# Attention over neighbour lists: the sums of a block's weights added by GpSimd in place of VectorE, with running least and greatest sums for the guard

## The chip, the cores and the metric

The kernel runs on one core of one Trainium2 chip. The metric is the device time of one execution in microseconds. A profiled execution gives the trace; the times are those of executions without a profile.

## The reference

Four graph layers run one after the other on the same graph of 2048 nodes (`adj` is a 0/1 matrix in which about one entry in 128 is set) and on 8 batch entries with 128 features per node. Layers 0 and 1 are multi-head attention over the neighbours with a feed-forward part; layers 2 and 3 are graph attention with additive scores. Only neighbours count in each softmax.

```python
# layers 0 and 1
Q = (h @ Wq).reshape(B, N, 8, 16); K = ...; V = ...
scores = jnp.einsum('bnhd,bmhd->bhnm', Q, K) / jnp.sqrt(16)
scores = jnp.where(adj == 0, -jnp.inf, scores)
attn = jax.nn.softmax(scores, axis=-1)
attn_out = jnp.einsum('bhnm,bmhd->bnhd', attn, V).reshape(B, N, 128)
x = layer_norm(h + (attn_out @ Wo + bo))
x = layer_norm(x + relu(x @ W1 + b1) @ W2 + b2)
# layers 2 and 3
h = x @ W
e = leaky_relu((h @ a_src)[:, :, None] + (h @ a_dst)[:, None, :], 0.2)
att = softmax(jnp.where(adj == 0, -jnp.inf, e), axis=-1)
x = layer_norm(att @ h + x)
```

## The kernel before

**Lists and blocks.** The kernel first finds each node's neighbours, sorts the nodes by their number of neighbours and cuts them into 16 blocks of 128 nodes, one node per partition. A block t has as many slots as its longest list may need (`CAPS`: 28 plus 2 folded ones for block 0, then 23, 21, 20, 19, 18, 18, 17, 16, 16, 15, 14, 14, 13, 12, 11). In each layer a table in HBM holds one row per node: key and value of all 8 batch entries in layers 0 and 1 (2048 columns), projected features and two exponentials in layers 2 and 3 (1040 columns). For slot k of block t, one indirect DMA of GpSimd's queue (`gather`, L319) fetches the table rows of the k-th neighbours of the block's 128 nodes into a buffer `kv`, of which there are six (`KVB`).

**Chunks.** The work is cut into chunks of 2 slots (layers 0 and 1) or 4 slots (layers 2 and 3). A chunk of attention goes through these steps in `attention_chunk`:

- VectorE multiplies the keys by the queries `q` (L640, 128 x 2048 elements) and adds halves of the products once or twice (L645);
- TensorE sums what is left into the PSUM tile `pair` (L648), and ScalarE takes the exponential into the weights `w`, 64 columns per slot (8 batch entries x 8 heads, L653);
- VectorE multiplies the values by the weights (L659);
- TensorE adds the weighted values of all slots into the PSUM accumulator `acc` (L326, through `add_up`). After that the buffer is free, and the gather of the chunk six places on may go.

**The sums.** The softmax needs the sum of `w` over a block's slots. When a block's last chunk is due to be weighted, `sums` calls `reciprocal_sums`, which adds the slots by halves on VectorE (L467, in place, the last step L469), adds the folded part in block 0, reduces the 64 sums to their least and greatest value (L476, L477, kept in one column of `dmin` and `dmax` per layer and block) and inverts them (L478). At the very end `verdict` reduces `dmin` and `dmax` and sets a flag; if a sum was out of bounds, a general path would compute everything anew. Layers 2 and 3 use the same function with one reduction (L471) over 8 columns.

**Order.** No scheduler moves instructions: the order in which the program is written is each engine's order. The main loop `layers` runs over the chunks i and interleaves three ages: products of chunk i, sums and weighting of chunk i-2, accumulation of chunk i-3. Between them it calls `slot()` three times a chunk. A slot moves every generator in `threads` and `tails` on by one `yield` and lets `fetch` issue gathers up to three chunks ahead (four in layers 2 and 3). So a chunk's gather stands on GpSimd's queue at the start of the round three chunks earlier.

`scales` (a thread begun right after the sums) spreads the inverted sums over the features on ScalarE and transposes them on TensorE. `tail` waits four slots (layers 0 and 1) after the last accumulation and then calls `outputs` (L678: accumulator times scale) and begins `attention_tail`: output projection, norm, feed-forward part, norm, and the next layer's rows. When both halves of a block are done, `state_done` writes the state back (SP's queue) and scatters the rows into the next layer's table (`put_rows`, L515, GpSimd's queue). The first chunks of the next layer use lists sorted such that they need only the first 13, 14 or 15 blocks of the new table (`EARLY`); all later ones need all 16, and `fetch` holds their gathers back until those writes have been issued. If a chunk's gather isn't issued when its turn comes, the loop calls empty slots until it is:

```python
            while i < len(every) and now[1] <= i:
                slot()
```

Of the kernel before, what the change touches and what calls it, by code (L numbers as in the profile page):

```python
# [8 lines left out]
F32 = mybir.dt.float32  # L9
# [5 lines left out]
ALU = mybir.AluOpType  # L15
AX = mybir.AxisListType

P = 128
B, N, D = 8, 2048, 128
NT = N // P  # L20
NH = 8
# [7 lines left out]
NB = 8  # L29
# [9 lines left out]
BASE, MANY, FOLD = 28, 16, 2  # L39
CAPS = [BASE + FOLD, 23, 21, 20, 19, 18, 18, 17, 16, 16, 15, 14, 14, 13, 12, 11]  # L40
# [44 lines left out]
def sparse_path(ctx: ExitStack, tc: tile.TileContext, ins: dict, out: bass.AP, flag: bass.AP):  # L85
# [10 lines left out]
    nc = tc.nc  # L96
    const = ctx.enter_context(tc.tile_pool(name="const", bufs=1))
    work = ctx.enter_context(tc.tile_pool(name="work", bufs=2))
    small = ctx.enter_context(tc.tile_pool(name="small", bufs=2))
# [5 lines left out]
    def misc():  # L105
        return pm.tile([P, 512], F32, tag="m", name="m")
# [51 lines left out]
    score = const.tile([P, 2, NT, 2 * B], F32, name="score")  # L158
    over = const.tile([P, 2, NT], F32, name="over")
    found = dram.tile([N, N // SEG * 8], F32, name="found")  # L160
    dmin = const.tile([P, 4, NT], F32, name="dmin")
    dmax = const.tile([P, 4, NT], F32, name="dmax")

# [159 lines left out]
    def turn_into(dst, src, start):  # L325
        nc.tensor.matmul(  # L326
            dst, src, ident, start=start, stop=True, is_transpose=True, skip_group_check=True
        )
# [127 lines left out]
        box["folded"] = small.tile([P, columns], F32, tag="folded", name="folded", bufs=1)  # L456
        nc.scalar.copy(box["folded"], ps)

    def reciprocal_sums(l, t, w, columns, folded):

        sums = small.tile([P, columns], F32, tag="sums", name="sums")
        n = CAPS[t] if t > 0 else BASE
        if l < 2:

            while n > 2:
                m = -(-n // 2)
                nc.vector.tensor_add(w[:, : n - m, :], w[:, : n - m, :], w[:, m:n, :])  # L467
                n = m
            nc.vector.tensor_add(sums, w[:, 0, :], w[:, 1, :])  # L469
        else:  # L470
            nc.vector.tensor_reduce(  # L471
                sums, w[:, :n, :].rearrange("p s c -> p c s"), axis=AX.X, op=ALU.add
            )
        if t == 0:
            nc.vector.tensor_add(sums, sums, folded)
        nc.vector.tensor_reduce(dmin[:, l, t : t + 1], sums, axis=AX.X, op=ALU.min)  # L476
        nc.vector.tensor_reduce(dmax[:, l, t : t + 1], sums, axis=AX.X, op=ALU.max)  # L477
        nc.vector.reciprocal(sums, sums)  # L478
        return sums

# [188 lines left out]
            yield  # L669

    def sums(l, t, box):
        box["r"] = reciprocal_sums(l, t, box["w"], NB * (NH if l < 2 else 1), box.get("folded"))

    def outputs(l, t, box):
        acc, scale = box["acc"], box["scale"]
        box["o"] = o = work.tile([P, NB, P], F32, tag="o", name="o", bufs=1)
        for i in range(0, NB, 4):
            nc.vector.tensor_mul(o[:, i : i + 4, :], acc[:, i : i + 4, :], scale[:, i : i + 4, :])  # L678

    def scales(l, box):  # L680

        box["scale"] = scale = work.tile([P, NB, P], F32, tag="oT", name="scale", bufs=1)
        if l < 2:
            r = box["r"].rearrange("p (b h) -> p b h", h=NH)
            nc.scalar.copy(
                scale.rearrange("p b (j h) -> p b j h", h=NH),
                r[:, :, None, :].to_broadcast([P, NB, HD, NH]),
            )
            yield
        for i in range(0, NB, 4):  # L690
            pt = misc()
            for j in range(4):
                r = box["r"][:, i + j : i + j + 1].to_broadcast([P, P])
                turn_into(pt[:, j * P : (j + 1) * P], scale[:, i + j, :] if l < 2 else r, j == 0)
            yield
            nc.scalar.copy(scale[:, i : i + 4, :].rearrange("p b n -> p (b n)"), pt)
# [378 lines left out]
    def verdict():  # L1075
        ok = small.tile([P, 5], F32, tag="ok", name="ok", bufs=1)
        every = score.rearrange("p a t b -> p (a t b)")
        nc.vector.tensor_reduce(ok[:, 3:4], every, axis=AX.X, op=ALU.max)
        nc.vector.tensor_reduce(ok[:, 4:5], every, axis=AX.X, op=ALU.min)
        nc.vector.tensor_single_scalar(ok[:, 3:4], ok[:, 3:4], SCORE_MAX, op=ALU.is_le)  # L1080
        nc.vector.tensor_single_scalar(ok[:, 4:5], ok[:, 4:5], -SCORE_MAX, op=ALU.is_ge)
        nc.vector.tensor_mul(ok[:, 3:4], ok[:, 3:4], ok[:, 4:5])
        nc.vector.tensor_reduce(ok[:, 0:1], dmin.rearrange("p a b -> p (a b)"), axis=AX.X, op=ALU.min)
        nc.vector.tensor_reduce(ok[:, 1:2], dmax.rearrange("p a b -> p (a b)"), axis=AX.X, op=ALU.max)
        nc.vector.tensor_reduce(ok[:, 2:3], over.rearrange("p a b -> p (a b)"), axis=AX.X, op=ALU.max)
        nc.vector.tensor_single_scalar(ok[:, 0:1], ok[:, 0:1], SUM_MIN, op=ALU.is_ge)
        nc.vector.tensor_single_scalar(ok[:, 1:2], ok[:, 1:2], SUM_MAX, op=ALU.is_le)
        nc.vector.tensor_single_scalar(ok[:, 2:3], ok[:, 2:3], 0.0, op=ALU.is_le)
        nc.vector.tensor_mul(ok[:, 0:1], ok[:, 0:1], ok[:, 1:2])
        nc.vector.tensor_mul(ok[:, 0:1], ok[:, 0:1], ok[:, 2:3])  # L1090
        nc.vector.tensor_mul(ok[:, 0:1], ok[:, 0:1], ok[:, 3:4])
        pk = misc()
        nc.tensor.matmul(pk[:1, :1], ok[:, 0:1], onesc, start=True, stop=True)
        bad = small.tile([1, 1], I32, tag="bad", name="bad", bufs=1)
        nc.vector.tensor_scalar(bad, pk[:1, :1], -1.0, float(P), op0=ALU.mult, op1=ALU.add)
        nc.sync.dma_start(flag, bad)
# [8 lines left out]
    for l in range(4):  # L1105
        per = 2 if l < 2 else 4
        for t, k, ns, folded in pieces(l, per):
            c = dict(l=l, t=t, k=k, ns=ns, folded=folded, box=blocks[l][t])
# [48 lines left out]
    def later(n, make):  # L1157
        for _ in range(n):
            yield
        yield from make()  # L1160

    def tail(l, t, box):
        for _ in range(4 if l < 2 else 3 if t > NT - 4 else 5):
            yield
        outputs(l, t, box)
        if l < 2:
            tails.append(later(1, lambda: attention_tail(l, t, box, 0)))
            tails.append(later(4, lambda: attention_tail(l, t, box, 4)))
        else:
            tails.append(later(1, lambda: gat_tail(l, t, box)))  # L1170
        yield
# [19 lines left out]
    def layers():  # L1191
# [9 lines left out]
        for i in range(len(every) + 2):  # L1201
            c1, c, n1, n2 = (chunk(i + j) for j in range(-1, 3))
            while added:
                c2 = added.pop(0)
                go(c2)
                if c2["last"]:
                    threads.append(tail(c2["l"], c2["t"], c2["box"]))
# [23 lines left out]
            if c1["l"] in (2, 3) and c1["last"]:  # L1231
                sums(c1["l"], c1["t"], c1["box"])
                threads.append(scales(c1["l"], c1["box"]))
# [6 lines left out]
            while weighed and len(weighed) > (2 if c["l"] in (0, 1) else 0):  # L1240
                c2 = weighed.pop(0)
                if c2["last"]:
                    sums(c2["l"], c2["t"], c2["box"])
                    threads.append(scales(c2["l"], c2["box"]))
                go(c2, 2)
                added.append(c2)
            if c1["l"] in (2, 3):
                go(c1, 2)
                if c1["last"]:
                    threads.append(tail(c1["l"], c1["t"], c1["box"]))  # L1250
            slot()
        verdict()
        drain()

# [528 lines left out]
```

## Time and profile before

| | us |
|---|---|
| median of 3 runs | 3161.54 |
| lowest and highest | 3149.05, 3168.8 |
| profiled execution, its own time | 3022.89 |
| span of its trace | 3021.1 |
| VectorE (DVE) busy in the span | 2743.3 |
| TensorE (PE) busy | 2517.4 |
| GpSimd (POOL) busy | 1784.3 |
| ScalarE (ACT) busy | 1379.7 |

The profiled execution was faster than all three timed ones. Durations below come from its trace. In a group of the profile, the columns are line, engine, operation, tiles, shapes and count, then the busy time in us and the mean of one in ns, then the engine's idle time before these instructions and what ended it. A row of a timeline has start, length, engine, line, operation, tiles, shapes and, in brackets, the idle time before it. L319 is line 319 of the kernel before. The attention layers take about 215 to 1140 us and 1140 to 2090 us of the span, and layers 2 and 3 the rest.

### The profile page before, as it was taken

The numbers are of one execution on the slowest core, as the hardware profiler recorded it, in microseconds if no ns is written. First come the engines' busy times: TensorE is split into PE (matmuls) and PEld (weight loads), VectorE is DVE, ScalarE is ACT, GpSimd is POOL, SyncE is SP. The second block draws the span as 40 slices with busy tenths as digits, with TensorE's granted clock in tenths as the row PEclk, the third lists the DMA queues.
The fourth block names the chain that finished last, engine by engine and source line by source line (L and its number), as shares of the span: only waits on it lengthen the run. The fifth ranks groups of instructions, "written<-read, shape, count | busy, mean of one in ns | idle before, by whom it ended". The sixth has DMA issues, their size and how long they took to land.

```text
span 3021.1 us, 52130 instructions
## 1 busy us (share of the span) xinstructions
PE 2517.4 (83%) x19258; PEld 2320.8 (77%) x19258; DVE 2743.3 (91%) x2945; ACT 1379.7 (46%) x4898; POOL 1784.3 (59%) x1293
## 2 busy tenths in 40 slices
PE   5756888789889999688888898999678898788886
PEld 3646777778788898677888788888578888687786
DVE  8788999999999998999999999998599998499996
ACT  4721333444445555043444454545345556244454
POOL 0057578677755644545546555554577775477773
PEclk8978999999999999899999999999798899899998
DMA  8688889988988887778888889886799999799995
GB/s 331 234 301 320 310 310 324 347 299 314 362 304 335 313 305 316 279 260 343 307 322 325 344 323 333 322 309 241 259 395 403 397 414 355 261 411 412 409 412 216
DMA packets 200692, 987.63 MB, mean 327 GB/s; under 512 B 31918, under 2 KB 33712, under 8 KB 128436
## 3 DMA queue, kind: packets, MB, share of 16 engines
q0 software_dynamic: 175024, 890.45, 77.7%
q1 hardware_dynamic: 20502, 75.52, 6.5%
q10 hardware_dynamic: 4904, 18.24, 1.9%
q8 instruction: 155, 2.54, 0.3%
q14 instruction: 107, 0.88, 0.1%
HBM read 937.16 MB, written 91.55 MB: 341 GB/s over the span
## 4 chain that ended last, share of the span: by engine, by line
PE 36%; DVE 30%; DMA 16%; issue 9%; ACT 5%; POOL 1%; POOLq 0%; DVEq 0%; ACTq 0%
PE acc L326 12%; DMA kv<-table,lists 11%; DVE kv L640 9%; DVE kv L659 8%; PE pair L648 5%; DVE kv L645 4%; DMA kv<-table,sorted_lists 3%; PE m L752 3%; DVE kv L797 3%; PE m L731 2%; PE m L533 2%; PE m L333 2%; DMA table<-rows,perm 2%; PE m L557 1%; PE m L548 1%
## 5 line engine op out<-in xcount | busy, mean ns | idle before, releaser
L319 POOL DMA_INDIRECT kv<-table,lists x955 | 1334.0, 1397 | 764.8 <-PE acc L326 491.9
L326 PE MATMUL acc<-ident,kv 128*128 128x128 f32 x8208 | 1059.8, 285 | 180.0 <-DVE kv L659 98.4
L326 PEld LDWEIGHTS acc<-ident,kv 128*128 128x128 f32 x8208 | 978.2, 148 | 258.7 <-DVE kv L659 120.5
L640 DVE TENSOR_TENSOR kv<-kv,q 128x2048 f32<-128x2048 f32 (+1 forms) x282 | 629.2, 2231 | 46.5 <-DMA kv<-table,lists 18.7
L659 DVE TENSOR_TENSOR kv<-kv,w 128x2048 f32<-128x2048 f32 (+1 forms) x284 | 632.4, 2227 | 0.0
L648 PE MATMUL pair<-kv,ident 128*128 128x128 f32 (+1 forms) x3344 | 444.3, 284 | 141.5 <-issue 66.7
L797 DVE TENSOR_TENSOR kv<-kv,pair 128x3584 f32<-128x3584 f32 (+1 forms) x150 | 540.0, 3600 | 1.9
L648 PEld LDWEIGHTS pair<-kv,ident 128*128 128x128 f32 x3344 | 411.7, 197 | 167.1 <-issue 100.3
L653 ACT ACTIVATE w<-pair,lmask 128x64 f32<-128x64 f32 x554 | 144.7, 311 | 738.8 <-PE pair L648 738.7
L645 DVE TENSOR_TENSOR kv<-kv 128x1024 f32<-128x1024 f32 (+1 forms) x434 | 442.5, 1020 | 14.3
L494 ACT ACTIVATE n<-m,eps 128x128 f32<-128x128 f32 x512 | 181.5, 367 | 296.8 <-PE m L718 154.3
L319 POOL DMA_INDIRECT kv<-table,sorted_lists x153 | 188.4, 1231 | 126.3 <-PE acc L326 56.6
L802 ACT ACTIVATE kv<-kv,ws 128x128 f32<-128x128 f32 x554 | 177.9, 400 | 180.6 <-DVE ws L791 173.9
L844 ACT ACTIVATE n<-m,eps 128x128 f32<-128x128 f32 x256 | 90.8, 374 | 183.1 <-PE m L836 183.1
L515 POOL DMA_INDIRECT table<-rows,perm x57 | 85.1, 1493 | 132.9 <-ACT score L568 31.4
L752 PE MATMUL m<-w_L_w,hT 128*128 128x128 f32 x1024 | 156.2, 275 | 0.0
L501 ACT ACTIVATE n<-m,rs 128x128 f32<-128x128 f32 x512 | 146.3, 376 | 1.1
L752 PEld LDWEIGHTS m<-w_L_w,hT 128*128 128x128 f32 x1024 | 134.9, 192 | 0.0
L731 PE MATMUL m<-n1T,w_L_gnn_W 128*128 128x512 f32 x256 | 131.5, 597 | 0.6 <-ACT q L606 0.6
L333 PE MATMUL m<-ident,n 128*128 128x128 f32 x640 | 107.8, 291 | 11.9 <-ACT rows L562 7.5
L678 DVE TENSOR_TENSOR o<-acc,scale 128x512 f32<-128x512 f32 x128 | 82.9, 683 | 37.6 <-PE acc L326 23.3
L333 PEld LDWEIGHTS m<-ident,n 128*128 128x128 f32 x640 | 83.4, 151 | 36.2 <-issue 14.7
(238 smaller groups left out, 3615.4 us busy)
## 6 DMA issues: line engine op xcount, KB each, us to landing
kept<-xT SPq DMA_DIRECT2D x48, 512.0 KB, 6.2
xT<-kept SPq DMA_DIRECT2D x48, 512.0 KB, 7.5
kv<-in_adj_dram SPq DMA_DIRECT2D x16, 1024.0 KB, 6.5
table<-kv ACTq DMA_DIRECT2D x16, 1024.0 KB, 5.7
kv<-table,lists POOLq DMA_INDIRECT x955, 8.6
kv<-in_x_nodes_dram SPq DMA_DIRECT2D x16, 512.0 KB, 12.5
kv<-table,sorted_lists POOLq DMA_INDIRECT x153, 6.9
found<-cand POOLq DMA_DIRECT2D x16, 64.0 KB, 4.3
```

What stands on the lines that cost most here:

```text
L319: nc.gpsimd.indirect_dma_start(out=dst, out_offset=None, in_=tables[l][:, :], in_offset=bass.IndirectOffsetOnAxis(ap=index, axis=0), bound ...
L326: nc.tensor.matmul(dst, src, ident, start=start, stop=True, is_transpose=True, skip_group_check=True)
L333: nc.tensor.transpose(pt[:, j * P : (j + 1) * P], src[:, j, :], ident)
L494: nc.scalar.activation(dst[:, i, :], z[:, i, :], AF.Square, bias=eps, scale=D**-0.5, accum_out=ss[:, i : i + 1],)
L640: nc.vector.tensor_mul(kk, kk, q[:, None].to_broadcast([P, ns, NB, D]))
L645: nc.vector.tensor_add(kk[:, :, :, :width], kk[:, :, :, :width], kk[:, :, :, width : 2 * width])
L648: nc.tensor.matmul(sc, ident, kk[:, :, :, j : j + NH], start=j == 0, stop=j + NH == width)
L659: nc.vector.tensor_mul(vv, vv, w[:, k : k + ns, :].rearrange("p s (b h) -> p (s b) h", h=NH)[:, :, None, :] .to_broadcast([P, ns * NB, HD, ...
L731: nc.tensor.matmul(ph, wt["1"][:, f * P : (f + 1) * P], n1T.rearrange("p b c -> p (b c)"), start=True, stop=True,)
L752: nc.tensor.matmul(y[:, j, :], hT[:, f, j, :], wt["2"][:, f, :], start=False, stop=f == 1, skip_group_check=True,)
L797: nc.vector.tensor_mul(hv[:, :, :nv, :], hv[:, :, :nv, :], wc[:, :, :nv, None].to_broadcast([P, ns, nv, D]))
L802: nc.scalar.mul(hv[:, i, b, :], hv[:, i, b, :], ws[:, i, b - nv : b - nv + 1])
```

## The change

For layers 0 and 1 the sums of the weights move to GpSimd: a new function `attention_sums` does the same additions by halves in the same order with GpSimd's `tensor_add`, on GpSimd's queue, where the gathers stand. It neither reduces nor inverts. Instead `scales` waits three slots and then does three operations on VectorE: it takes the element-wise minimum of the 64 sums with a tile `least`, the maximum with a tile `most`, and the reciprocal. `least` and `most` start at 1 and run over all blocks of both layers. In `verdict` they are merged into the smaller `dmin` and `dmax`, which layers 2 and 3 still fill as before. `tail` waits seven slots in place of four in layers 0 and 1.

```diff
-    dmin = const.tile([P, 4, NT], F32, name="dmin")
-    dmax = const.tile([P, 4, NT], F32, name="dmax")
+    dmin = const.tile([P, 2, NT], F32, name="dmin")
+    dmax = const.tile([P, 2, NT], F32, name="dmax")
+    least = const.tile([P, NB * NH], F32, name="least")
+    most = const.tile([P, NB * NH], F32, name="most")
+    nc.vector.memset(least, 1.0)
+    nc.vector.memset(most, 1.0)
...
-    def reciprocal_sums(l, t, w, columns, folded):
-
-        sums = small.tile([P, columns], F32, tag="sums", name="sums")
+    def attention_sums(t, w, folded):
+
+        sums = small.tile([P, NB * NH], F32, tag="sums", name="sums")
         n = CAPS[t] if t > 0 else BASE
-        if l < 2:
-
-            while n > 2:
-                m = -(-n // 2)
-                nc.vector.tensor_add(w[:, : n - m, :], w[:, : n - m, :], w[:, m:n, :])
-                n = m
-            nc.vector.tensor_add(sums, w[:, 0, :], w[:, 1, :])
-        else:
-            nc.vector.tensor_reduce(
-                sums, w[:, :n, :].rearrange("p s c -> p c s"), axis=AX.X, op=ALU.add
-            )
+        add = nc.gpsimd.tensor_add
+        while n > 2:
+            m = -(-n // 2)
+            add(w[:, : n - m, :], w[:, : n - m, :], w[:, m:n, :])
+            n = m
+        add(sums, w[:, 0, :], w[:, 1, :])
+        if t == 0:
+            add(sums, sums, folded)
+        return sums
+
+    def reciprocal_sums(l, t, w, folded):
+
+        sums = small.tile([P, NB], F32, tag="sums", name="sums")
+        n = CAPS[t] if t > 0 else BASE
+        nc.vector.tensor_reduce(
+            sums, w[:, :n, :].rearrange("p s c -> p c s"), axis=AX.X, op=ALU.add
+        )
         if t == 0:
             nc.vector.tensor_add(sums, sums, folded)
-        nc.vector.tensor_reduce(dmin[:, l, t : t + 1], sums, axis=AX.X, op=ALU.min)
-        nc.vector.tensor_reduce(dmax[:, l, t : t + 1], sums, axis=AX.X, op=ALU.max)
+        nc.vector.tensor_reduce(dmin[:, l - 2, t : t + 1], sums, axis=AX.X, op=ALU.min)
+        nc.vector.tensor_reduce(dmax[:, l - 2, t : t + 1], sums, axis=AX.X, op=ALU.max)
         nc.vector.reciprocal(sums, sums)
         return sums
...
     def sums(l, t, box):
-        box["r"] = reciprocal_sums(l, t, box["w"], NB * (NH if l < 2 else 1), box.get("folded"))
+        if l < 2:
+            box["r"] = attention_sums(t, box["w"], box.get("folded"))
+        else:
+            box["r"] = reciprocal_sums(l, t, box["w"], box.get("folded"))
...
     def scales(l, box):
 
+        if l < 2:
+            for _ in range(3):
+                yield
+            nc.vector.tensor_tensor(least, least, box["r"], op=ALU.min)
+            nc.vector.tensor_max(most, most, box["r"])
+            nc.vector.reciprocal(box["r"], box["r"])
...
+        dmin2, dmax2 = (d.rearrange("p a b -> p (a b)") for d in (dmin, dmax))
+        nc.vector.tensor_tensor(dmin2, dmin2, least[:, : 2 * NT], op=ALU.min)
+        nc.vector.tensor_tensor(dmin2, dmin2, least[:, 2 * NT :], op=ALU.min)
+        nc.vector.tensor_tensor(dmax2, dmax2, most[:, : 2 * NT], op=ALU.max)
+        nc.vector.tensor_tensor(dmax2, dmax2, most[:, 2 * NT :], op=ALU.max)
...
     def tail(l, t, box):
-        for _ in range(4 if l < 2 else 3 if t > NT - 4 else 5):
+        for _ in range(7 if l < 2 else 3 if t > NT - 4 else 5):
             yield
```

## The prediction

> **What bounds the kernel now.** I read the page's busy totals first, then busy time by stage, then VectorE's groups with shapes kept apart, then VectorE's waits, and last the timelines of VectorE and GpSimd beside each other.
>
> ```profile
> PE 2517.4 (83%) x19258; PEld 2320.8 (77%) x19258; DVE 2743.3 (91%) x2945; ACT 1379.7 (46%) x4898; POOL 1784.3 (59%) x1293
> ...
> 215.00:1140.00 925.00, 795.63 (x6077) 727.25 (x6077) 892.51 (x796) 396.25 (x1356) 618.08 (x364) 0.97 0.86 319
> 1140.00:2090.00 950.00, 839.67 (x6624) 774.14 (x6623) 893.27 (x660) 408.46 (x1534) 508.59 (x298) 0.97 0.83 311
> ```
>
> The two rows are the two attention layers (columns: stretch, length, PE, PE loads, DVE, ACT, POOL, clock, DMA share, GB/s). VectorE is busy 892.5 of 925 us and 893.3 of 950 us, 96% and 94%. TensorE follows at 86% and 88%, the DMA engines at 86% and 83%. So VectorE sets the pace there, with two others 8 to 12 points behind. VectorE's waits in this stretch say the same: the largest row is 20.5 us in 16 waits for gathered rows, the next 14.0 us.
>
> ```profile
> L659 DVE TENSOR_TENSOR kv<-kv,w 128x2048 f32<-128x2048 f32 x270 | 616.2, 2282 | 0.0
> L640 DVE TENSOR_TENSOR kv<-kv,q 128x2048 f32<-128x2048 f32 x268 | 612.1, 2284 | 46.5 <-DMA kv<-table,lists 18.7 <-DMA kv<-table,sorted_lists 13.8 <-ACT q L606 13.3
> ...
> L478 DVE RECIPROCAL sums<-sums 128x64 f32<-128x64 f32 x32 | 17.7, 553 | 1.1
> ...
> L469 DVE TENSOR_TENSOR sums<-w 128x64 f32<-128x64 f32 x32 | 7.2, 225 | 1.1
> ...
> L476 DVE TENSOR_REDUCE dmin<-sums 128x1 f32<-128x64 f32 x32 | 7.0, 220 | 1.1
> L477 DVE TENSOR_REDUCE dmax<-sums 128x1 f32<-128x64 f32 x32 | 6.7, 209 | 0.0
> ```
>
> These are the products that fill VectorE, and the small operations that the change touches. All the products have two inputs in SBUF. Whether that matters to GpSimd is to be seen where GpSimd's gathers (POOL) stand beside VectorE:
>
> ```profile
> 1018.53 2.23 DVE L659 TENSOR_TENSOR kv<-kv,w 128x2048 f32<-128x2048 f32 x1
> 1020.68 2.28 DVE L640 TENSOR_TENSOR kv<-kv,q 128x2048 f32<-128x2048 f32 x1
> 1024.86 2.28 DVE L659 TENSOR_TENSOR kv<-kv,w 128x2048 f32<-128x2048 f32 x1
> 1027.06 2.28 DVE L640 TENSOR_TENSOR kv<-kv,q 128x2048 f32<-128x2048 f32 x1
> ...
> 1019.22 2.39 POOL L319 DMA_INDIRECT kv<-table,lists  x1 [2.25 <-PE acc L326]
> 1025.35 2.66 POOL L319 DMA_INDIRECT kv<-table,lists  x1 [1.53 <-PE acc L326]
> ...
> 2166.12 3.89 DVE L797 TENSOR_TENSOR kv<-kv,pair 128x3584 f32<-128x3584 f32 x1
> 2167.67 0.99 POOL L319 DMA_INDIRECT kv<-table,sorted_lists  x1 [0.30 <-PE acc L326]
> 2168.97 0.99 POOL L319 DMA_INDIRECT kv<-table,sorted_lists  x1 [0.30 <-issue]
> ```
>
> The first two gathers start in the middle of a product and end at 1021.61 and 1028.01, which is 0.93 and 0.95 us after the *next* VectorE instruction began (1020.68, 1027.06). They stood still until the running product was over. The last two run under a product whose second input, `pair`, lies in PSUM, and take 0.99 us. Counted over 240 to 2090 us, 328 of the 552 gathers take over 1.2 us, and 278 of these end 0.82 to 0.98 us after a VectorE start. So a GpSimd instruction that reads SBUF waits out a VectorE product with two SBUF inputs.
>
> **What the Trainium skill says.** "SBUF — State Buffer", section "Who interferes with whom": a VectorE instruction with two SBUF inputs contends with a GpSimd instruction that reads SBUF; the one that starts first keeps the shared read port for the whole instruction and the other is blocked. The trace agrees for VectorE first (above). It has no long GpSimd read, so the other direction is not shown. "GPSIMD Engine Reference", section 3.1: an fp32 add of 2048 elements takes 4497 ns on GpSimd, about 2.6 cycles at 1.2 GHz per element, 2293 ns on VectorE. The trace has 2284 ns for VectorE and no add on GpSimd. "Perfetto Trace Analysis", section "Optimizing Scalar/DVE Operations", warns that moving work between these two might not help as they share a read port.
>
> **The change part by part.**
>
> *Removed from VectorE.* 32 blocks (2 layers, 16 blocks). The rows of L467 (112 adds, 64 to 896 columns, 225 to 1096 ns) sum to 50.7 us; with L469's 7.2 the tree costs 57.9 us. The two reductions to one column cost 7.0 + 6.7 = 13.7 us.
>
> *Added to VectorE.* A running minimum and maximum of 64 columns per block: 64 instructions like L469's 225 ns, 14.4 us. The reciprocal stays (553 ns), three rounds later. The guard's four operations at the end and two fills at the start are under 2 us. Net 57.9 + 13.7 - 14.4 = 57.2 us off VectorE, 1.8 us a block.
>
> *Added to GpSimd.* 146 adds. A block of n neighbours needs n-1 sums of 64 columns; over the 16 sizes (275 neighbours) that is 259 x 64 x 2 = 33,152 elements per partition. At 2.17 ns (2.6 cycles, an estimate from GPSIMD Engine Reference) 72 us, and for each instruction 60 ns (what 4497 ns leaves) to 250 ns: 81 to 108 us in all, about 2.9 us a block. GpSimd idles 33% and 46% in these layers, so there is room.
>
> *What the adds do to VectorE.* This cost is unknown. From below: zero, if VectorE does not stand still for them; then the 57.2 us are a gain. From above: the whole 81 to 108 us, since 94 to 96% of VectorE's time is filled, mostly with two-input products. I take the block to hold in both directions, as the page says, and 95 us, of which a tenth falls on VectorE's idle time or on operations with one SBUF input: 86 us. Net on VectorE: 86 - 57 = +29 us.
>
> *Waiting at the running minimum.* On GpSimd the adds stand between the gathers of chunk i+3 and of chunk i+4. They come when VectorE starts the weighting (L659) of chunk i-2. VectorE reaches the new minimum after L659, L640, one or two L645 and L659: 2.28 x 3 + 1.6 = 8.4 us. The chain needs 4 or 5 turns, each waiting for the product in progress and then adding: four turns take about 2.2 + 2.3 + 1.4 + 2.3 for the products and 2.7 for the adds, 10.9 us against 8.4 + 2.5 (VectorE stands for the same adds). It is about even; a fifth add finishes while VectorE waits at the minimum, 0.3 us. Behind that wait stand the next L640 and everything after it. I take 0.3 x 32 = 10 us; 0 to 60.
>
> *Gathers behind the adds.* The gather of chunk i+4 (free to go at 1019.2 in the example) goes some 7 us later, when the adds end. It lands 8.6 us after its issue (page, part 6), about 1037 to 1040, and its product starts at 1041.65. That just fits; bounds 0 and 3 us a block (96 us). I take 0.
>
> *Three rounds more before the tail.* Scaling and outputs come three rounds (one chunk) later in each block. Inside a layer this is only latency. At the layer ends the new rows of the last blocks are awaited: VectorE idles 5.28 us at 1237 and 18.36 us at 2160 until a gather that follows the last table write (1224.94 and 2147.35). Each grows by one chunk, 6.3 us (L640 + L645 + L659) and 5.6 us (L797 + L808 + 0.5). Counted in the program's own loop, the empty rounds before that second gather rise from 3 to 12. Sum +12 us. On GpSimd's queue the table writes and the gathers of x fall one chunk later against the gathers; SP's order does not change.
>
> *Sum.* 29 + 10 + 12 = +51 us on the profiled execution (3022.89 us), so 3074. The median of the runs is 3161.54, 4.6% above that execution; I put the same 51 us on it: 3213 us.
>
> **The rivals.**
>
> *B, the adds do not hold VectorE.* GpSimd has the room. Then VectorE loses 57 us, the layer ends cost 12: -45 us, 3117. TensorE at 86 to 88% and DMA at 83 to 86% may keep some back, so 3117 to 3150. The point: as long as the adds hold VectorE for less than 57 - 12 = 45 of their 95 us, the kernel gains. For it: no row of before shows VectorE standing for a gather. Against: a gather reads one index per partition, too short to show it. Chance 0.22.
>
> *C, the gathers fall behind.* One mechanism: the chain of adds, taking turns with the products, keeps GpSimd's in-order queue for over 11 us a block, and chunk i+4's rows land after they are wanted. It decides from about 11 us on (1041.65 - 8.6 - two gathers of 2.4 = 1028, against 1017 for the start). At 3 us a block it adds 96 us: 3310; at half that 3260. Against: GpSimd catches up, its 46% of idle time in the second layer. Chance 0.2.
>
> *D, no net difference.* The adds hold the port for only part of their time (about 50 of 95 us): 50 - 57 + 12 and up to 10 at the minimum, 3165 to 3177. Chance 0.15.
>
> **How the numbers follow.** The forecast has 0.43, the rivals 0.22, 0.2 and 0.15. The forecast's own range is 3190 to 3245. The range that holds 8 in 10 reaches from B's bulk, 3120, to C's lower half, 3280. A measurement of this kernel tells about 1% (32 us) from no change. Faster by more than that: three quarters of B, 0.17. Within: the rest of B, D and the lower edge of the forecast, 0.23. Slower: 0.60.
>
> **What would show it.** In the trace after: L640 and L659 longer than 2.28 us, or gaps before them, where GpSimd adds; each add starting at the end of a VectorE product; GpSimd's adds near 95 us in sum; a wait of VectorE at the minimum under 1 us a block; the waits for `table2` rows near 24 us. If the products keep 2.28 us with no gaps, B is right. If VectorE's waits for `lists` rise from 20.5 us to about 100, it is C.

## The result and the profile after

The changed kernel takes 3241.40 us (median of 6 runs) where the kernel before takes 3165.77 us: 2.5% slower, ratio 1.0251 (95% interval 1.0223 to 1.0279). A second comparison of the same two kernels on another chip gave 3125.84 us against 3023.39 us, ratio 1.0326 (1.0304 to 1.0348). Chips differ: on some the kernel before takes about 3030 us, on others about 3150 us, and the trace of before shown above came from one of the first kind. So ratios below are within one chip, and traces are set beside each other only where both kernels ran on chips of one kind, or the text says otherwise. Two runs, slower than the others of their kernel, are left out of the numbers below: 4018.84 us at a granted clock of 0.62 in the last experiment, and 3199.34 us with the adds on VectorE.

Two such traces are the kernel before once more and the changed kernel once more (L650, L655 and L669 are the former L640, L645 and L659, L323 is the gather, L691 the output product). The rows give busy time by stage: attention layers 0 and 1, then layer 2; columns as in the prediction. The first three rows are of before:

```profile
177.90:1132.60 954.70, 809.09 (x6158) 741.40 (x6159) 920.43 (x833) 394.64 (x1351) 644.18 (x378) 0.96 0.87 322
1132.60:2090.80 958.20, 842.60 (x6598) 776.70 (x6597) 894.86 (x654) 407.84 (x1531) 495.25 (x293) 0.96 0.82 308
2090.80:2571.00 480.20, 394.51 (x3039) 371.33 (x3038) 417.47 (x481) 255.34 (x1013) 329.24 (x299) 0.90 0.94 362
```

and these of the changed kernel:

```profile
177.10:1176.20 999.10, 839.72 (x6131) 769.59 (x6132) 903.63 (x763) 390.33 (x1336) 681.02 (x446) 0.91 0.83 307
1176.20:2154.20 978.00, 857.90 (x6601) 789.69 (x6600) 884.37 (x582) 406.35 (x1531) 551.02 (x370) 0.94 0.81 302
2154.20:2664.20 510.00, 403.48 (x3093) 377.89 (x3092) 416.33 (x478) 262.27 (x1043) 329.30 (x300) 0.90 0.89 341
```

The attention layers grew by 64.2 us (999.1 + 978.0 against 954.7 + 958.2), layer 2 by 29.8, layer 3 by nothing (461.7 us in both). Against the trace of before that stands ahead of the prediction (953.3 + 947.3 us) the attention layers grew by 76.5 us: two executions of one kernel differ by 12 us there. In the attention layers VectorE is busy 27 us *less* (1788.0 against 1815.3) and idle 91 us more. What fills the idle time stands in VectorE's groups, here of the first trace of the changed kernel (a chip of the other kind), shapes kept apart:

```profile
L669 DVE TENSOR_TENSOR kv<-kv,w 128x2048 f32<-128x2048 f32 x270 | 632.4, 2342 | 0.0
...
L698 DVE TENSOR_TENSOR least<-least,sums 128x64 f32<-128x64 f32 x32 | 7.2, 225 | 120.7 <-POOL sums L472 116.5 <-POOL sums L474 4.2
L699 DVE TENSOR_TENSOR most<-most,sums 128x64 f32<-128x64 f32 x32 | 7.0, 219 | 0.0
```

VectorE waits 120.7 us, 3.8 us a block, at the running minimum for GpSimd's last add (116.4 us in the second trace). The weighting products went from 2282 to 2342 ns: they are held, but only a little. Summed over all VectorE instructions of the attention layers, the time above the median of each instruction's form is 26 us (29 in the second trace) against 1 us before. This sum is what "held" means below. One size of GpSimd's adds, in the same trace:

```profile
L470 POOL TENSOR_TENSOR w<-w 128x128 f32<-128x128 f32 x24 | 18.6, 777 | 1.9
```

All 146 adds take 139.7 us; at the shortest length of each size (0.32 us for 64 columns, 1.14 for 448, 2.08 for 896) it would be 97 us. The rest, 43 us, comes where adds run beside VectorE's products: those above take 777 ns on average, 453 undisturbed. Two blocks show both parts. In the first, VectorE and then GpSimd:

```profile
1069.69 2.77 DVE L655 TENSOR_TENSOR kv<-kv 128x1024 f32<-128x1024 f32 x2
1072.38 2.67 DVE L669 TENSOR_TENSOR kv<-kv,w 128x2048 f32<-128x2048 f32 x1
1075.81 0.23 DVE L698 TENSOR_TENSOR least<-least,sums 128x64 f32<-128x64 f32 x1 [0.75 <-POOL sums L472]
...
1070.54 4.84 POOL L470 TENSOR_TENSOR w<-w 128x448 f32<-128x448 f32 x3
```

The pair of L655 takes 2.77 us in place of 1.95, the product 2.67 in place of 2.28: here adds hold VectorE for 1.2 us. In the other block nothing is held, and VectorE stands still:

```profile
457.88 2.28 DVE L669 TENSOR_TENSOR kv<-kv,w 128x2048 f32<-128x2048 f32 x1
468.94 0.23 DVE L698 TENSOR_TENSOR least<-least,sums 128x64 f32<-128x64 f32 x1 [8.78 <-POOL sums L472]
...
458.46 2.60 POOL L323 DMA_INDIRECT kv<-table,lists  x1 [0.30 <-issue]
461.37 1.00 POOL L323 DMA_INDIRECT kv<-table,lists  x1 [0.31 <-issue]
462.67 1.00 POOL L417 DMA_INDIRECT place<-ranks,lists  x1 [0.30 <-issue]
463.98 0.97 POOL L344 DMA_INDIRECT xs<-in_x_nodes_dram,perm  x1 [0.30 <-issue]
464.97 3.54 POOL L470 TENSOR_TENSOR w<-w 128x640 f32<-128x640 f32 x4
468.59 0.32 POOL L472 TENSOR_TENSOR sums<-w 128x64 f32<-128x64 f32 x1
```

When VectorE comes to the minimum (460.16), GpSimd is issuing one DMA and has three more ahead of the adds. The adds themselves then run undisturbed.

### The profile page after: what moved, and what is told of

Same layout as the page of the kernel before. It is cut to its first block, busy times and chain, and to the rows that moved or that the text cites. A ratio compares the mean times of both kernels' runs of the same rounds, so it can differ in the third digit from the quotient of the medians.

```text
span 3241.3 us, 52176 instructions
## 1 busy us (share of the span) xinstructions
PE 2634.5 (81%) x19258; PEld 2404.9 (74%) x19258; DVE 2715.9 (84%) x2805; ACT 1377.8 (43%) x4898; POOL 1867.7 (58%) x1439
## 5 line engine op out<-in xcount | busy, mean ns | idle before, releaser
L323 POOL DMA_INDIRECT kv<-table,lists x955 | 1309.1, 1371 | 866.3 <-PE acc L330 515.6
L330 PE MATMUL acc<-ident,kv 128*128 128x128 f32 x8208 | 1093.2, 288 | 194.0 <-issue 84.5
L330 PEld LDWEIGHTS acc<-ident,kv 128*128 128x128 f32 x8208 | 997.9, 150 | 281.7 <-issue 153.9
L650 DVE TENSOR_TENSOR kv<-kv,q 128x2048 f32<-128x2048 f32 (+1 forms) x282 | 627.5, 2225 | 55.5 <-DMA kv<-table,lists 23.9
L669 DVE TENSOR_TENSOR kv<-kv,w 128x2048 f32<-128x2048 f32 (+1 forms) x284 | 649.6, 2288 | 0.0
L658 PE MATMUL pair<-kv,ident 128*128 128x128 f32 (+1 forms) x3344 | 465.2, 293 | 145.3 <-issue 73.5
L658 PEld LDWEIGHTS pair<-kv,ident 128*128 128x128 f32 x3344 | 432.6, 206 | 167.3 <-issue 110.2
L655 DVE TENSOR_TENSOR kv<-kv 128x1024 f32<-128x1024 f32 (+1 forms) x434 | 452.7, 1043 | 14.3
L323 POOL DMA_INDIRECT kv<-table,sorted_lists x153 | 187.7, 1227 | 132.6 <-PE acc L330 52.7
L337 PE MATMUL m<-ident,n 128*128 128x128 f32 x640 | 120.7, 299 | 26.6 <-ACT n L871 12.3
L827 DVE TENSOR_TENSOR kv<-kv 128x1024 f32<-128x1024 f32 x75 | 91.5, 1220 | 59.2 <-ACT kv L821 56.4
```

Source lines behind the costliest of these rows:

```text
L323: nc.gpsimd.indirect_dma_start(out=dst, out_offset=None, in_=tables[l][:, :], in_offset=bass.IndirectOffsetOnAxis(ap=index, axis=0), bound ...
L330: nc.tensor.matmul(dst, src, ident, start=start, stop=True, is_transpose=True, skip_group_check=True)
L337: nc.tensor.transpose(pt[:, j * P : (j + 1) * P], src[:, j, :], ident)
L650: nc.vector.tensor_mul(kk, kk, q[:, None].to_broadcast([P, ns, NB, D]))
L655: nc.vector.tensor_add(kk[:, :, :, :width], kk[:, :, :, :width], kk[:, :, :, width : 2 * width])
L658: nc.tensor.matmul(sc, ident, kk[:, :, :, j : j + NH], start=j == 0, stop=j + NH == width)
```

## The experiments

Three readings stood at the start: the wait at the minimum is the cost (W); the adds cost VectorE their own time wherever they fall (H); the later tails are the cost (L). The gain or loss of each run is against the kernel before on the same chip. The times expected in the first four were worked out from 3166 us for the kernel before, which takes 3150.83 us on their chip, so the ratios decide.

**The minimum one chunk later.**

```diff
         if l < 2:
-            for _ in range(3):
+            for _ in range(6):
                 yield
...
     def tail(l, t, box):
-        for _ in range(7 if l < 2 else 3 if t > NT - 4 else 5):
+        for _ in range(8 if l < 2 else 3 if t > NT - 4 else 5):
```

> The changed kernel with the running minimum three slots (one chunk) later: scales waits 6 slots in place of 3, tail 8 in place of 7. In the trace of the changed kernel VectorE waits 120.7 us at the minimum for GpSimd's last add, and its products and adds are lengthened by only about 24 us. Theory W (the wait is the cost, GpSimd comes late to its adds): the wait falls to under 15 us and nothing takes its place: about 3241 - 110 = 3130 us. Rival H (the adds cost VectorE their own time wherever they fall; before, most of them fell into the wait): with VectorE busy, the products are lengthened by 60 to 97 us in place of 24: 3241 - 110 + 35 to 75 = 3165 to 3205 us. Rival L (the later tail and the layer ends are the cost): one slot more of tail, so as slow as the changed kernel or slower, 3240 to 3250.

Measured 3225.15 us, ratio 1.0244 (1.0196 to 1.0292). VectorE's waits in the attention layers, first of the changed kernel, then of this one (who waits, for whom, then us in total, times, longest):

```profile
DVE least L698 <- POOL sums L472: 106.5, 27, 8.8
DVE kv L650 <- DMA kv<-table,lists: 29.6, 12, 5.7
...
DVE kv L650 <- DMA kv<-table,lists: 65.6, 38, 5.6
DVE least L698 <- POOL sums L472: 26.9, 18, 3.8
DVE o L691 <- ACT scale L715: 18.0, 23, 3.4
```

The wait at the minimum shrank to 27 us in these layers, and the time did not follow. The waits for gathered rows more than doubled, the scales came late, and the held time rose from 26 to 44 us. Neither W (3130 us) nor H (3165 to 3205) is met: the lateness moved. By its ratio the kernel is as slow as the changed one, as L had it; what the later tails cost by themselves is measured below.

**The adds ahead of the gather.**

```diff
-            box["r"] = attention_sums(t, box["w"], box.get("folded"))
+            if "r" not in box:
+                box["r"] = attention_sums(t, box["w"], box.get("folded"))
...
             now[0] = i
+            if weighed and weighed[0]["last"] and len(weighed) > (1 if c["l"] in (0, 1) else 0):
+                c2 = weighed[0]
+                c2["box"]["r"] = attention_sums(c2["t"], c2["box"]["w"], c2["box"].get("folded"))
             fetch()
```

> The changed kernel with the adds issued at the start of the round, ahead of the gather of chunk i+3 on GpSimd's queue and not behind it; everything else as changed. Theory W: GpSimd no longer stands behind a gather that waits for an accumulation, so the adds end before VectorE reaches the minimum; the wait falls from 120.7 us to under 30 and the time to 3241 - 95 = 3145 us. Rival H: the adds now meet products, whose lengthening rises from 24 to 60 to 97 us: 3180 to 3220 us. A gather that comes late behind the adds would show as a longer wait of VectorE for kv than before (20.5 us in the list gathers of before).

Measured 3265.00 us, ratio 1.0352 (1.0303 to 1.0401), the slowest of all and slower than W and H had it. Waits of this kernel in the attention layers (L699 is the minimum here):

```profile
DVE kv L650 <- DMA kv<-table,lists: 101.3, 52, 6.4
DVE least L699 <- POOL sums L472: 22.1, 18, 5.8
```

The adds now begin 3.2 us after the weighting of their chunk has begun, in place of 8.8, and the wait at the minimum has shrunk to 22 us, as W said. But what stands behind them is the gather, and VectorE waits 101.3 us for its rows; 54 us are held. With the run before, this shows that W alone is wrong: GpSimd's queue is late, and whoever is second in it is waited for.

**The adds alone, with nobody waiting for them.** The sums stay on VectorE as before; beside them GpSimd does the same number of adds, of the same sizes, on a tile of its own.

```diff
+            k = n
+            while k > 2:
+                m = -(-k // 2)
+                nc.gpsimd.tensor_add(shadow[:, : k - m, :], shadow[:, : k - m, :], shadow[:, : k - m, :])
+                k = m
+            nc.gpsimd.tensor_add(shadow[:, 0, :], shadow[:, 0, :], shadow[:, 0, :])
...
```

> The kernel before, its sums still on VectorE, and beside them on GpSimd's queue the same number of adds with the same column counts on a private tile of zeros, for whose result nobody waits. Theory W: an add that nobody waits for costs only what it holds VectorE in the changed kernel, about 24 us: 3166 + 24 = 3190 us. Rival H: the adds hold VectorE for nearly their whole uncontended time of 97 us: 3240 to 3265 us. If adds and products don't contend at all: 3166 us.

Measured 3212.10 us, ratio 1.0199 (1.0157 to 1.0240): 61 us, between W (+24) and H (+74 to 99). 43 us are held time, and waits for list rows are 65.2 us. The same kernel on a chip of the other kind:

> The shadow adds once more (144 adds beside the sums on VectorE, nobody waits for them), on one chip with the changed kernel, because the fills (+0.6%) and the few shadow adds (+1.5%) ran on another chip than the first shadow adds (+2.0%). Expected if the chip does not matter to the ratio: +1.9 to 2.1%, with VectorE lengthened by about 43 us and some 30 us of idle time more in the attention layers. If the late gathers were that chip's: nearer to +1.5%.

Measured 3095.12 us, ratio 1.0234 (1.0217 to 1.0251), again 43 us held. So adds that give VectorE nothing to wait for still cost 61 to 72 us.

**The kernel before, once more**, to tell the chips apart.

> The kernel before, once more, for a trace whose layers 2 and 3 are like those of the other traces: in the first trace of before they took 480 and 463 us, in the traces since 540 to 584 and 511 to 519, though no edit touches them. Expected of all theories: the attention layers again 953 and 947 us (within 5), layers 2 and 3 together 1050 to 1105 us.

One run, 3034.58 us. Layers 2 and 3 took 480.2 and 461.7 us, not the 1050 to 1105 together that was expected: the difference came with the chip. The two runs of the shadow adds show the same, 1056.5 us for these layers on one chip and 945.2 on the other. The second attention layer took 958.2 us where 947 (within 5) was expected.

**The same queue time without reads.** Each shadow add became two fills.

```diff
...
-                nc.gpsimd.tensor_add(shadow[:, : k - m, :], shadow[:, : k - m, :], shadow[:, : k - m, :])
+                for _ in range(2):
+                    nc.gpsimd.memset(shadow[:, : k - m, :], 0.0)
```

> The kernel before, and at the places of the shadow adds GpSimd writes zeros instead: two fills of the same columns for each add, which occupy its queue for about as long (some 88 us in all by the fill of 64 columns at 141 ns and of 128 at 204 ns, against 97 us of adds) and read nothing from SBUF. Shadow adds cost +73 us in the attention layers (43 us of lengthened VectorE instructions and 30 us more idle time). Theory P (the read port is behind both parts: adds hold VectorE, and VectorE's products hold the adds, so that these take 220 us of GpSimd's queue in place of 97 and make gathers late): fills cost next to nothing, 0 to 12 us. Rival Q (GpSimd's queue is too full for 90 us more of whatever work): VectorE is not lengthened but its waits for gathered rows grow as with the adds, +25 to 35 us.

Measured 3050.69 us against 3030.85, ratio 1.0063 (1.0040 to 1.0087): 20 us, between P and Q. GpSimd's work and VectorE's weighting product in this kernel, then in the second run of the shadow adds:

```profile
L470 POOL MEMSET shadow<- 128x64 f32 (+11 forms) x288 | 84.3, 293 | 14.7
L667 DVE TENSOR_TENSOR kv<-kv,w 128x2048 f32<-128x2048 f32 x270 | 616.6, 2284 | 0.0
...
L469 POOL TENSOR_TENSOR shadow<-shadow 128x128 f32<-128x128 f32 (+10 forms) x112 | 170.9, 1525 | 7.1
L471 POOL TENSOR_TENSOR shadow<-shadow 128x64 f32<-128x64 f32 x32 | 48.6, 1518 | 2.5
L667 DVE TENSOR_TENSOR kv<-kv,w 128x2048 f32<-128x2048 f32 x270 | 629.8, 2333 | 0.0
```

84 us of fills hold nothing (2284 ns) and cost 20 us through later gathers (waits for list rows 51.6 us against 25.0 before). The adds, whose shortest lengths sum to 83 us, occupy GpSimd for 219.5 us, hold VectorE for 43 and cost 72. An add of 64 columns that takes 0.29 us alone takes 1.52 us between the products. So VectorE and GpSimd hold each other up, and the reading of SBUF, with what it adds to the queue time, makes up some 50 of the 72 us; 84 us of queue time without reads make up 20.

**The same columns in fewer adds**, 52 in place of 144.

```diff
         if l < 2:
+            for k in split(n - 1, BASE // 2):
+                nc.gpsimd.tensor_add(shadow[:, :k, :], shadow[:, :k, :], shadow[:, :k, :])
```

> The shadow adds with the same columns in fewer instructions: one or two a block, 52 in place of 144; about 80 us of uncontended adds in place of 97. If the cost goes by instruction (each add waits out a product, then VectorE waits for it): a good third of the lengthening and of the late gathers, +20 to 30 us in place of +61. If it goes by the columns read: VectorE is held for most of 80 us, more per add than before, and the cost stays at +50 to 70 us.

Measured 3073.37 us, ratio 1.0147 (1.0120 to 1.0174): 42.5 us, between the two. The adds:

```profile
L467 POOL TENSOR_TENSOR shadow<-shadow 128x512 f32<-128x512 f32 (+7 forms) x52 | 90.9, 1748 | 2.4
```

They take 90.9 us of GpSimd in place of 219.5, and gathers are late by little (waits for list rows 37.6 us against 61.9 with 144 adds). But 50 us are held, 7 more. In these two runs the held time goes with the columns, the delay of GpSimd's queue with the number of adds.

**The delays alone.** The changed kernel with the adds on VectorE (`add = nc.vector.tensor_add`), then the same with `range(0)` in `scales` and 4 in `tail`.

> The changed kernel with the adds back on VectorE; the running minimum and maximum, the three slots of scales and the seven slots of tail stay. Theories W and H: what is left of the change is +0.7 us on VectorE and the later layer ends, so 3166 + 1 + about 12 = 3179 us (3166 to 3190). Rival L: the delay of the tail is what costs, so about 3241 us.

> The changed kernel with the adds on VectorE and the delays taken back (scales without its three slots, tail with four): what is left is running minimum and maximum in place of the two reductions. With the delays this cost +0.8%. If the delays at the layer ends are that cost: no difference to before, +0.7 us by count (ratio 1.000, within 0.003). If minimum and maximum over shared tiles cost it: again about +0.8%.

Measured 3179.75 us, ratio 1.0079 (1.0056 to 1.0103), and 3038.66 us, ratio 1.0023 (1.0013 to 1.0032). Running minimum and maximum cost 7 us, where 0.7 was counted, and the slots in `scales` and `tail` about 0.56% more, 17 us; the two kernels ran on chips of different kinds, so this difference is rough. L is a small part.

**The changed kernel once more.**

> The changed kernel once more, unedited, for its ratio and trace beside the shadow adds on the same chip: +2.5% again, about 120 us of waiting at the running minimum, 26 us of lengthened VectorE instructions. If this chip is one where the kernel before takes 3031 us, the absolute time is about 3107 us.

3125.84 us, ratio 1.0326; wait at the minimum 116.4 us, held 29 us. The ratio is above the +2.5% that was expected; the stages above are of this run.

**The sums on TensorE**, to take them off the shared port.

```diff
-        add = nc.gpsimd.tensor_add
-        while n > 2:
...
+        ps = misc()[:, : NB * NH]
+        for i in range(n):
+            nc.tensor.matmul(ps, ident, w[:, i, :], start=i == 0, stop=i == n - 1)
+        nc.scalar.copy(sums, ps)
...
```

> The changed kernel with the sums on TensorE: one product with the identity per slot, 550 in all, accumulated in PSUM and copied to SBUF by ScalarE; minimum, maximum and delays as changed. [...] Theory P: VectorE loses its 57 us, nothing holds its products, and the delays cost their 0.8%: 57 - 25 = 32 us less than before (-1.0%), if TensorE, busy 88% in the attention layers, takes 550 x 0.17 us = 94 us more without becoming the bound. If TensorE becomes the bound (88% + 5%, with its accumulations later and the buffers freed later): +0 to +40 us.

3112.54 us, ratio 1.0297 (1.0277 to 1.0317): 89 us, more than either case expected. Nothing is held (2 us), but the sums take 126.6 us of TensorE (1100 products of 275 ns in the trace, where 550 of 170 were counted). TensorE is busy 1773 of 1966 us in the attention layers, and VectorE waits 89.0 us at the minimum:

```profile
DVE least L696 <- ACT sums L470: 89.0, 23, 7.7
DVE kv L646 <- DMA kv<-table,lists: 50.8, 36, 5.5
```

> The sums on TensorE with the running minimum one chunk later: scales waits 6 slots in place of 3, tail 8 in place of 7. With the minimum after 3 slots this version cost +3.0%, VectorE waited 89 us at the minimum for ScalarE's copy of the sums (so for TensorE, which comes late), and no product was lengthened. Theory W (the wait is a cost of its own): it goes, 57 us of VectorE work stay away, and the later layer end costs some 20 to 30: 3112 - 75 = 3035 to 3040 us where before takes 3023 (+0.5%), at best level with it. Theory S (whoever is late stays late: without the wait VectorE runs ahead and waits for gathered rows instead, whose buffers TensorE's late accumulations free): waits for kv rise from 51 to over 100 us and the time stays within 1% of +3.0%.

3227.85 us against 3152.16, ratio 1.0211 (1.0160 to 1.0263). The wait at the minimum is gone (3.5 us). The waits for list rows hardly rose (57.5 us), but VectorE waits 64.7 us for the scales in the same layers: with tail at 8 the output product follows them at once. So W's +0.5% is refuted; S, within 1% of +3.0%, holds in its sum but not in the place that it named.

No version beats the kernel before.

One thing more differs, and no run isolates it: in the attention layers the changed kernel was granted a TensorE clock of 0.91 and 0.94, the kernel before 0.96 in both (rows above). The lower clock does not explain the loss. On one chip the kernel with the adds on VectorE had 0.90 to 0.91 over whole runs and lost 0.8%, the one with the later minimum had 0.91 to 0.92 and lost 2.4%; TensorE's accumulating products took 286 ns in layer 0, against 282 before. Whether it adds to the loss is open.

## Why the prediction was right, and where not

The forecast was slower, +51 us; the measurement is +76 us on that chip, inside the range, and +102 us on the other. The direction is right, but the forecast's reason for it is not what made the kernel slower, and that the sum came out near is luck. The decisive cost was to be the hold of VectorE by the adds, 86 us against 57 us saved. The hold is 26 to 29 us, less than the 45 us below which rival B had the kernel gain; with that term alone put right, the prediction's sum is -57 + 28 + 10 + 12 = -7 us. Two terms were missed, by about 58 us one way and 106 the other. The time went to VectorE's wait at the minimum, which stood in the sum at 10 us, and the first two experiments show GpSimd's late queue behind it: with the wait made small, the time stayed. That reading adds and VectorE's products stand in each other's way is borne out, by 72 us for adds where fills of like length cost 20 (two chips of one kind), but in kernels where nobody waits for the adds. Term by term:

- *Removed and added on VectorE* (-57.2 us): right. L698 and L699 take 7.2 + 7.0 us (14.4 predicted).
- *Adds on GpSimd* (81 to 108 us): 97 us undisturbed. Right.
- *Adds hold VectorE* (86 us): 26 to 29 us. Wrong in the changed kernel because most adds ran while VectorE stood at the minimum; with the minimum later, the same adds take 220 us and hold 44. Where nobody waits it was 43 us for 144 adds and 50 for 52, 52% and 74% of their shortest lengths (83 and 68 us), where the prediction took nine tenths. "SBUF — State Buffer", section "Who interferes with whom", calls the shared port pair an exclusive lock. Its words on the whole instruction stand at VectorE's two-port modes, and the prediction carried them over to adds that hold a product. That the two contend, and that fills do not, agrees with that section; that an add keeps VectorE out for its whole length does not fit these sums. Which part of an add does is open.
- *Waiting at the minimum* (10 us, 0 to 60): 116 to 121 us, outside the bounds, and the step that failed. It said that the adds come when VectorE starts the weighting of chunk i-2, and took the gather that is free to go at 1019.22 for that of chunk i+4. Counted through the queue it is the first of two gathers of chunk i+3, which stand *ahead* of the adds. Here is the second, and VectorE's first addition of that block's sums:

```profile
1016.03 1.36 DVE L467 TENSOR_TENSOR w<-w 128x448 f32<-128x448 f32 x3
...
1021.92 1.90 POOL L319 DMA_INDIRECT kv<-table,lists  x1 [0.31 <-issue]
```

The gather ends at 1023.82, 5.3 us after the weighting has begun (1018.53), and over 31 blocks of the trace of before 4.7 us after it on average. In the changed kernel the adds begin 8.8 us after the weighting and last 4.6 us; VectorE is at the minimum after 9.7 us and waits 3.7 (averages of 30 blocks). Of the shift from 4.7 to 8.8 us, 2.8 are the very work that was taken away: in before, the additions, the reductions and the reciprocal stand right ahead of the weighting on VectorE (2.83 us a block from L467 to L659), so without them VectorE comes sooner and GpSimd does not. All of this but the length of the adds and the other 1.3 us of the shift could be read from the trace of before.
- *Gathers behind the adds* (0 us): nearly so in the changed kernel, where VectorE's own wait gives the gathers time: waits for list rows 34.3 us in the attention layers against 25.0. In the kernels with as many adds and without most of that wait it is 62 to 101 us. Rival C had the late queue right, but not the place: the changed kernel waits for the adds.
- *Layer ends* (+12 us): too small. The delays cost about 17 us by the two runs on it. In layer 2, which grew by 29.8 us, the wait for the first gather that needs the whole table rose by 15.4 us (5.6 predicted), and the last block's wait at the minimum (11.0 us) falls into it too. First of before, then of the changed kernel:

```profile
DVE kv L785 <- DMA kv<-table,lists: 18.9, 1, 18.9
...
DVE kv L804 <- DMA kv<-table,lists: 34.3, 1, 34.3
DVE least L698 <- POOL sums L472: 11.0, 1, 11.0
```

Put together for the attention layers of the two traces of one kind: -57 us of work, +28 held, +105 at the minimum (116.4 less the 11.0 in layer 2), and -14 on other waits, which the wait at the minimum hides, make +62 of the 64 us. Rival B (-45 us) and D (no difference) are out by the time, though the hold was as small as B needed. Two of the signs that the prediction named did not come: adds near 95 us in sum (139.7) and a wait at the minimum under 1 us a block (3.8). Its count of long gathers is a little off and its reading stands: in the trace of before 539 gathers start between 240 and 2090 us, 337 take over 1.2 us, and 319 of these end 0.82 to 0.98 us after a VectorE start.

Open is why the same change costs 2.5% on one kind of chip and 3.3% on the other; the traces of before are of one kind only.

## What to carry to other kernels

An offloaded sum costs what its consumer waits for, and on an in-order queue that is settled by what stands ahead of it: count through the queue which transfer that is, and when it was released in the trace, before assuming that the engine is free because its idle share is high. Work given to an idle engine can still cost its neighbour: here GpSimd's adds, with nobody waiting for them, held VectorE for 43 to 50 us, and the additions take VectorE itself 58. Work that is taken away from just ahead of the consumer brings the consumer forward, and whoever took the work over has less time. When a wait is moved and the time stays, the late engine is the cost, not the place where it is waited for.

## What was not expected of the hardware

A short GpSimd add suffers most between VectorE products with two SBUF inputs: 64 columns take 0.29 us alone and 1.52 us on average there. In two runs held time went with the columns read (43 us for 144 adds, 50 us for 52 of the same columns), not with the number of instructions.
